# Block ends of a graph attention: the residual comes through an adding transfer instead of a VectorE pass

## The chip, the cores and the metric

The kernel runs on one core of a Trainium2 chip. The metric is device time in microseconds (us) of one execution. Before the change three runs took 1257.01, 1259.73 and 1262.62 us, with a median of 1259.73. One execution was also recorded by the hardware profiler, with the start and end of every instruction and DMA packet.

The engines are named as in the profile: PE is TensorE (matmuls), PEld its weight loads, DVE is VectorE, ACT is ScalarE, POOL is GpSimd and SP is SyncE, which here only issues transfers. Each engine works through its own queue in order.

## The reference

One layer has two parts. The first is a graph attention over N = 4096 nodes with 4 heads of 64 columns, the second a mixture of 8 experts with the best two for each node.

```python
h = einsum('nd,hdk->hnk', x, W)                      # x is layer-normed first
e = leaky_relu(s_row[:, :, None] + s_col[:, None, :], 0.2)
e = where(adj[None] > 0, e, -9e15)
out = einsum('hij,hjk->hik', softmax(e), h)          # then heads side by side: N x 256
residual = x @ Wr + br
y = elu(out) + residual
y = gamma * (y - mean(y)) / sqrt(var(y) + 1e-5) + beta
x = x + y                                            # then layer norm, top-2 gate, experts, x + sum
```

The change concerns the line `y = elu(out) + residual` and the row totals that the following layer norm needs. The exponential linear unit is written as max(y, 0) + exp(-relu(-y)) - 1; the -1 is already in the stored residual.

## The kernel before, in words

The rows of the attention are worked in four blocks a = 0 to 3 of 1024 rows, each in two halves of 512. Within a block a loop over j = 0 to 31 runs over 128 neighbours at a time. In each step VectorE makes four weight tiles `w` of 128x1024 (L1689, one per head, 10 buffers), ScalarE makes the mask (L1606) from an adjacency tile loaded by SP, and TensorE adds up 16 products for the rows (`acc`, L1198) and 8 for the softmax denominators (`den`, L1207), each recorded as two matmuls, so 48 records a step.

When a block's sums are complete, `finish_blocks` (L1393) ends it: divide by the denominators, the unit, the residual, two layer norms, storing the rows, choosing experts, and writing the rows into lists per expert in HBM (L1385, 16 scatters on POOL). It is a generator: each `next(pending)` (L1739) runs it up to the next `yield`, once for each step j of the following block. So the end of blocks 0, 1 and 2 lies spread over the loops a = 1, 2 and 3. The last block is ended by another function in the expert stage, which the change leaves alone. With the 26 yields of a block end (29 for the first block), of which one is taken at the block's boundary, the last piece with the scatters is traced at step 25 (28).

A scheduler orders each engine's queue ahead of time, by a cost model, from the order of tracing as priority and from readiness. TensorE's attention and block-end work is tied to the order of tracing by `queue` (L529) through `order_of` (L543); the other engines' work may be moved.

Tiles come from pools with a fixed number of buffers: `loaded` (L239) has two, `large` (L233) three. In a block end `rb` (the residual rows, loaded on SP by L1417) and later `xf` (x plus beta, L1439 to L1441) take turns in `loaded`; `y` of both halves and the scratch `m` are the three of `large`. There are adding transfers in the kernel already: L1441 adds x from HBM to a copy of beta, and L1450 adds `xf` to `y` within SBUF.

In loop a = 3 three more things matter. At step 3 `plan_early` (L1744) puts many small VectorE instructions beside the end of block 2. The expert stage starts behind the loop, with the first tile's rows already loaded at step 3. Its next rows, `early` (L571, from `load_full`, L1997), are loaded by SP once the lists are written, and transposed on TensorE (L607) before the products of the stage's first job (L1907) go on. `fetch` (L1777) loads each job's bias (L1792) and weights (L600, L1799) on the same SP queue.

Of the kernel before, what the change touches and what calls it, by code (L numbers as in the profile page):

```python
# [13 lines left out]
AF = mybir.ActivationFunctionType  # L14
OP = mybir.AluOpType
# [29 lines left out]
def gat_then_moe(  # L45
# [19 lines left out]
    nc = tc.nc  # L65
# [8 lines left out]
    HB = 2  # L74
# [34 lines left out]
    residual = nc.dram_tensor("residual", [N, D], F32, kind="Internal").ap()  # L109
# [39 lines left out]
    def rows_of(mat, b):  # L149
        return mat[ts(b, B), :].rearrange("(t p) d -> p t d", p=P)  # L150
# [50 lines left out]
    def sums_of(name, n=TB):  # L201
        return small.tile([P, n], F32, tag=name, name=name)

    def squares(square, src, off, junk):

        for t in range(TB):
            nc.scalar.activation(  # L207
                junk[:, t, :], src[:, t, :], AF.Square, bias=off[:, t : t + 1],
                accum_out=square[:, t : t + 1],
            )  # L210

    def means(total):

        off = sums_of("off", HB * TB)
        nc.vector.tensor_scalar(off, total, -1.0 / D, None, op0=OP.mult)  # L215
        return off


    def forward(apart, stack):
# [13 lines left out]
        def large(name):  # L233
            return home[0].tile([P, TB, D], F32, tag="large", name=name, bufs=3)
# [4 lines left out]
        def loaded(name):  # L239
            return fin.tile([P, TB, D], F32, tag="loaded", name=name, bufs=2)  # L240
# [4 lines left out]
        def bank(shape, name):  # L245
            return ps.tile(shape, F32, tag="bank", name=name, bufs=3)
# [296 lines left out]
        def order_of(ins):  # L543

            if ordered[0] or strict[0]:
                queue(ins)
            return ins.ins
# [67 lines left out]
        with ExitStack() as layer:  # L615
# [620 lines left out]
            def shares_of(pd):  # L1236

                z = small.tile([P, TB, H, HB], F32, tag="z", name="z")
                for h in range(0, H, 2):
                    nc.vector.reciprocal(z[:, :, h : h + 2], pd[:, :, PLACE[h] : PLACE[h] + 2, :HB])  # L1240
                return z
# [151 lines left out]
            def finish_blocks(a):  # L1393

                u = fin.tile([P, HB, H // 2, B], F32, tag="u", name="u", bufs=1)
                ud = fin.tile([P, B], F32, tag="ud", name="ud", bufs=1)

                nc.scalar.activation(ud, den, AF.Identity, bias=tiny)
                for i in reversed(range(H // 2)):
                    for half in range(HB):  # L1400
                        nc.scalar.activation(  # L1401
                            u[:, half, i], acc[half][i], AF.Identity, bias=hbar[:, i : i + 1]
                        )
                yield
                pd = bank([P, TB, H, Q], "pd")
                for t in range(TB):
                    order_of(nc.tensor.transpose(
                        pd[:, t].rearrange("p h q -> p (h q)"), ud[:, ts(t, P)], ident
                    ))
                z = shares_of(pd)  # L1410
                xe = rows_listed()
                n = HB * TB
                halves = [(half, slice(half * TB, (half + 1) * TB)) for half in range(HB)]
                rbs, ys, xbs = [], [], []
                for half, here in halves:
                    rbs.append(loaded("rb"))
                    nc.sync.dma_start(rbs[-1], rows_of(residual, a * HB + half))  # L1417
                for half, here in halves:
                    ys.append(large("y"))
                    results_of(ys[half], u[:, half], z[:, :, :, half])  # L1420
                    yield
                m = large("m")
                total = sums_of("total", n)
                for half, here in halves:
                    y = ys[half]
                    nc.scalar.activation(m, y, AF.Relu, scale=-1.0)
                    nc.scalar.activation(m, m, AF.Exp, scale=-1.0)
                    nc.vector.scalar_tensor_tensor(y, y, 0.0, m, op0=OP.max, op1=OP.add)
                    for t in range(TB):
                        nc.vector.scalar_tensor_tensor(  # L1430
                            y[:, t, :], y[:, t, :], 0.0, rbs[half][:, t, :], op0=OP.add, op1=OP.add,
                            accum_out=total[:, half * TB + t : half * TB + t + 1],
                        )
                    yield
                off = means(total)
                square = sums_of("square", n)
                for half, here in halves:
                    squares(square[:, here], ys[half], off[:, here], m)
                    xbs.append(loaded("xf"))  # L1439
                    nc.scalar.copy(xbs[half], bet.unsqueeze(1).to_broadcast([P, TB, D]))  # L1440
                    nc.gpsimd.dma_start(xbs[half], rows_of(x, a * HB + half), accum_op=OP.add)  # L1441
                    yield
                r = rstd_of(square, n, 1.0 / D)
                nc.vector.tensor_tensor(off, off, r, OP.mult)
                yield
                for half, here in halves:
                    y = ys[half]
                    normal(y, y, off[:, here], r[:, here])
                    nc.vector.tensor_tensor(y, y, gam.unsqueeze(1).to_broadcast([P, TB, D]), OP.mult)
                    nc.gpsimd.dma_start(y, xbs[half], accum_op=OP.add)  # L1450
                    yield
                yield
                total = sums_of("total", n)
                for half, here in halves:
                    for t in range(TB):
                        nc.scalar.activation(
                            m[:, t, :], ys[half][:, t, :], AF.Identity,
                            accum_out=total[:, half * TB + t : half * TB + t + 1],
                        )
                    nc.gpsimd.dma_start(rows_of(out, a * HB + half), ys[half])  # L1460
                    yield
                off = means(total)
                square = sums_of("square", n)
                for half, here in halves:
                    squares(square[:, here], ys[half], off[:, here], m)
                    yield
                r = rstd_of(square, n, 1.0 / D)
                nc.vector.tensor_tensor(off, off, r, OP.mult)
                yield
                for half, here in halves:  # L1470
                    normal(xe[:, here, :D], ys[half], off[:, here], r[:, here])
                    yield
                yield from route_rows(a * HB, xe)

            def rows_listed():
                return fin.tile([P, HB * TB, RW], F32, tag="xe", name="xe", bufs=1)

            def normal(into, src, off, r):

                for t in range(TB):  # L1480
                    nc.scalar.activation(
                        into[:, t, :], src[:, t, :], AF.Identity,
                        bias=off[:, t : t + 1], scale=r[:, t : t + 1],
                    )

            def results_of(y, u, z):

                pts = [bank([P, 2, HK], "ptr") for t in range(0, TB, 2)]
                for t in range(TB):
                    for i in range(H // 2):  # L1490
                        order_of(nc.tensor.transpose(  # L1491
                            pts[t // 2][:, t % 2, ts(i, P)], u[:, i, ts(t, P)], ident
                        ))
                for t in range(TB):
                    for h in range(H):
                        nc.scalar.activation(
                            y[:, t, ts(h, K)], pts[t // 2][:, t % 2, ts(h, K)], AF.Copy,
                            scale=z[:, t, h : h + 1],
                        )
# [110 lines left out]
            if not apart:  # L1610

                with tc.tile_pool(name="gen", bufs=2) as work:
# [12 lines left out]
                    for b in range(NB):  # L1625
# [4 lines left out]
                        for j in range(NT):  # L1630
# [6 lines left out]
                            for h in range(H):  # L1637
                                nc.vector.scalar_tensor_tensor(
                                    top[:, h, :], off, eb[:, j, h : h + 1], top[:, h, :],
                                    op0=OP.add, op1=OP.max,  # L1640
# [5 lines left out]
                            mx, mx, SLOPE, mx, op0=OP.mult, op1=OP.max  # L1646
                        )
                        for j in range(NT):
# [7 lines left out]
                            for h in range(H):  # L1656
                                nc.vector.tensor_scalar(
                                    w[:, h, :], rows[:, h, :], eb[:, j, h : h + 1], None,
                                    op0=OP.add,
                                )  # L1660
                            nc.vector.scalar_tensor_tensor(
                                w, w, SLOPE, w, op0=OP.mult, op1=OP.max
# [7 lines left out]
                        if b % HB == HB - 1 and b + 1 < NB:  # L1670
                            for _ in finish_blocks(b // HB):
                                pass
# [437 lines left out]
```

## Time and profile before

| what | value |
|---|---|
| profiled execution, whole time | 1258.36 us |
| its span, first to last instruction | 1256.7 us |
| median of three runs | 1259.73 us |
| TensorE busy | 1239.8 us (99%) |
| VectorE busy | 845.1 us (67%) |
| ScalarE busy | 448.2 us (36%) |
| GpSimd busy | 241.3 us (19%) |
| w tiles of VectorE, L1689 | 496 of 1.275 us |
| mean HBM traffic | 148 GB/s |

The attention loops a = 1, 2 and 3 run from about 250 to 777 us in the profile, the expert stage from 777 to the end. In a row of the profile, "x6: 1214/1222/1224" gives the count and the least, median and greatest duration in ns. Some rows name what ended an engine's idle time before an instruction. A window row gives the length of a stretch and then each engine's busy time in it with its count of instructions, the granted TensorE clock, the busy share of the DMA engines and GB/s. The chain of waits is the list of pieces that ended last, followed back from the last instruction: start, length, what. A busy TensorE row can include waiting within overlapping matmuls, so busy time alone doesn't tell the rate.

### The profile page before, as it was taken

The page shows a single profiled execution, that of the slowest core. Times are in us where ns is not written, and L with a number is a line of the kernel's source. Part 1 is how long each engine was busy: PE and PEld are TensorE (multiplying, and loading weights), DVE is VectorE, ACT ScalarE, POOL GpSimd, SP SyncE. Part 2 cuts the span into 40 slices and gives each one's busy share as a digit, 9 for nine tenths or more (in the row PEclk, how much of TensorE's full clock was granted, in tenths as well). Part 3 has the DMA queues.
Part 4 walks back from the last instruction along what each step waited for, and adds up shares of the span by engine and source line. Part 5 has one row for each costly group of instructions (what it writes and reads, how often), then busy time and mean ns, then how long its engine had stood idle before and what let it go on. Part 6 is the DMA issues. An engine that isn't in the chain of part 4 may idle for free.

```text
span 1256.7 us, 22720 instructions
## 1 busy us (share of the span) xinstructions
PE 1239.8 (99%) x8872; PEld 647.8 (52%) x8872; DVE 845.1 (67%) x1566; ACT 448.2 (36%) x918; POOL 241.3 (19%) x217
## 2 busy tenths in 40 slices
PE   9999999999999999999999999999999999999997
PEld 5444444332232332332325334888888876666686
DVE  7998887879999989999999996845111211111120
ACT  4332322265522375322655232533332332222322
POOL 4000000001002601006110024135222212122222
PEclk9999999999999999999999999999999999999999
DMA  6333533436533646335375423868898897455662
GB/s 215 118 119 110 167 111 102 157 113 139 181 110 107 224 116 201 107 98 157 112 171 191 122 84 103 269 181 230 218 234 213 215 229 144 106 139 106 138 161 36
DMA packets 155541, 190.23 MB, mean 151 GB/s; under 512 B 72312, under 2 KB 125680, under 8 KB 155040
## 3 DMA queue, kind: packets, MB, share of 16 engines
q1 hardware_dynamic: 133392, 145.39, 39.8%
q0 software_dynamic: 20544, 36.74, 13.2%
q10 hardware_dynamic: 1488, 6.55, 1.4%
q8 instruction: 71, 1.16, 0.4%
q14 instruction: 46, 0.38, 0.1%
HBM read 155.77 MB, written 29.74 MB: 148 GB/s over the span
## 4 chain that ended last, share of the span: by engine, by line
PE 93%; DVE 3%; issue 1%; ACT 1%; DMA 1%; another core or an unknown queue 0%; POOLq 0%; SPq 0%; DVEq 0%; ACTq 0%
PE acc L1198 33%; PE po L1907 18%; PE ph L1873 17%; PE den L1207 17%; PE pr L1053 2%; DVE w L1689 2%; PE ph L1101 2%; PE ptx L1253 0%; DMA early<-lists 0%; PE acc L894 0%; PE pt L780 0%; PE ptr L1491 0%; PE po L1946 0%; PE pl L1264 0%; PE po L875 0%
## 5 line engine op out<-in xcount | busy, mean ns | idle before, releaser
L1198 PE MATMUL acc<-w,ha 128*32 128x512 f32 x4096 | 669.9, 593 | 1.3 <-ACT u L1401 0.9
L1689 DVE SCALAR_TENSOR_TENSOR w<-er,eb,am 128x1024 f32<-128x1024 f32 x496 | 606.1, 1275 | 31.1 <-PE den L1207 31.1
L1207 PE MATMUL den<-w,unit 128*2 128x512 f32 x2048 | 466.9, 592 | 0.1
L1198 PEld LDWEIGHTS acc<-w,ha 128*32 128x32 f32 x4096 | 184.5, 110 | 292.8 <-issue 253.9
L1606 ACT ACTIVATE am<-adj 128x1024 bf16<-128x1024 int32 x124 | 130.6, 1054 | 346.5 <-DVE w L1689 211.7
L1873 PE MATMUL ph<-xT,w 128*128 128x256 f32 (+5 forms) x864 | 231.4, 425 | 2.9 <-ACT hT L1877 2.6
L1907 PE MATMUL po<-w,hT 128*128 128x256 f32 (+1 forms) x1040 | 230.2, 380 | 0.0
L1877 ACT ACTIVATE hT<-ph,bias 128x256 f32<-128x256 f32 (+5 forms) x216 | 111.1, 517 | 292.8 <-issue 185.7
L1907 PEld LDWEIGHTS po<-w,hT 128*128 128x128 f32 (+1 forms) x1040 | 196.2, 189 | 31.5 <-issue 3.1
L1873 PEld LDWEIGHTS ph<-xT,w 128*128 128x128 f32 x864 | 163.8, 191 | 63.4 <-issue 38.7
L1920 DVE SCALAR_TENSOR_TENSOR o<-po,share,b2s 128x256 f32<-128x256 f32 (+2 forms) x66 | 31.5, 479 | 230.1 <-PE po L1907 186.4
L1207 PEld LDWEIGHTS den<-w,unit 128*2 128x2 f32 x2048 | 93.5, 85 | 148.2 <-issue 139.8
L1932 POOL DMA_INDIRECT out<-o,ids x66 | 102.3, 1550 | 325.0 <-DMA out<-o,ids 151.0
L1385 POOL DMA_INDIRECT lists<-xe,at x64 | 89.0, 1391 | 268.0 <-issue 184.8
L1857 DVE STREAM_TRANSPOSE xT<-xr 128x512 f32<-128x512 f32 (+5 forms) x21 | 17.9, 851 | 57.1 <-PE ph L1873 31.2
L1053 PE MATMUL pr<-wr,xT 128*128 128x256 f32 x128 | 30.4, 381 | 0.2 <-ACT er L1147 0.2
L1895 ACT ACTIVATE b2s<-b2b,share 128x256 f32<-128x256 f32 x68 | 30.0, 498 | 0.0
L1121 POOL DMA_DIRECT2D residual<-rb x6 | 4.7, 784 | 121.2 <-DVE rb L1068 121.2
L1441 POOL DMA_DIRECT2D xf<-in_x x6 | 8.1, 1351 | 102.2 <-ACT xf L1440 102.2
L1053 PEld LDWEIGHTS pr<-wr,xT 128*128 128x128 f32 x128 | 24.1, 190 | 5.4 <-issue 0.9
L1101 PE MATMUL ph<-wall,xT 128*128 128x264 f32 x96 | 24.6, 399 | 0.0
L207 ACT ACTIVATE m<-y,off 128x256 f32<-128x256 f32 x48 | 23.7, 495 | 1.1 <-DVE off L215 0.6
(394 smaller groups left out, 617.9 us busy)
## 6 DMA issues: line engine op xcount, KB each, us to landing
adj<-in_adj SPq DMA_DIRECT2D x126, 512.0 KB
w<-in_L_ffn_W SPq DMA_DIRECT2D x54, 1024.0 KB
er<-parts ACTq DMA_DIRECT2D x3, 2048.0 KB
lists<-zeros POOLq DMA_DIRECT2D x8, 520.0 KB
residual<-rb POOLq DMA_DIRECT2D x8, 512.0 KB
rb<-residual SPq DMA_DIRECT2D x8, 512.0 KB
out<-y POOLq DMA_DIRECT2D x8, 512.0 KB
xb<-in_x SPq DMA_DIRECT2D x7, 512.0 KB
```

The costliest lines, as they stand in the source:

```text
L1053: order_of(nc.tensor.matmul(pr[:, k, :], turned[b][:, c, ts(t0 + k, P)], wr[:, c, :], start=(c == 0), stop=(c == DC - 1),))
L1101: order_of(nc.tensor.matmul(phs[t - t0], xT[:, c, ts(t, P)], wall[:, c, :], start=(c == 0), stop=(c == DC - 1),))
L1198: queue(nc.tensor.matmul(acc[half][h // 2][here : here + Q, :], ha[:, j, h * K + g * Q : h * K + (g + 1) * Q], w[half][h], start=(j == 0), ...
L1207: queue(nc.tensor.matmul(den[here : here + HB, :], unit[:, j, h, 1 - half : 1 - half + HB], w[half][h], start=(j == 0 and half == 0), stop ...
L1385: ins = nc.gpsimd.indirect_dma_start(lists, bass.IndirectOffsetOnAxis(ap=at[:, k, t : t + 1], axis=0), xe[:, t, :], None,).ins
L1606: nc.scalar.activation(am, at, AF.Relu, scale=2.0)
L1689: marks["w"] = nc.vector.scalar_tensor_tensor(wh[:, these], er[:, these, h], eb[:, j, h : h + 1], mask[:, these], op0=OP.max, op1=OP.min,).ins
L1873: order_of(nc.tensor.matmul(ph, job["w1"][:, c, ts(f, P)], xT[:, c, :], start=(c == 0), stop=(c == DC - 1),))
L1877: job["gelu"] = nc.scalar.activation(hT[:, f, :], ph, AF.Gelu, bias=job["bias"][:, f : f + 1]).ins
L1907: order_of(nc.tensor.matmul(po[:size], hT[:, f, k * CH : k * CH + size], w2[:, f, :], start=(f == 0), stop=(f == FC - 1),))
L1920: given_out.append(nc.vector.scalar_tensor_tensor(o[:size], po[:size], share[:size, k : k + 1], b2s[k][:size], op0=OP.mult, op1=OP.add,).ins)
L1932: added.append(add().ins)
```

## The change

Each half's exponential is made in a tile of its own from `loaded`, and a DMA issued on GpSimd adds the residual rows from HBM to it. Then four row passes of VectorE compute max(y, 0) plus that tile and take the row totals in the same instruction. The SP loads of `rb` and the VectorE pass over the whole half that put the unit together are gone. The making of the exponentials and the row passes are now two loops with a yield in each turn, where before they were one: two yields more per block end. `m`, still the scratch of the later square sums, is taken after them.

```diff
-                rbs, ys, xbs = [], [], []
-                for half, here in halves:
-                    rbs.append(loaded("rb"))
-                    nc.sync.dma_start(rbs[-1], rows_of(residual, a * HB + half))
+                ms, ys, xbs = [], [], []
                 for half, here in halves:
                     ys.append(large("y"))
                     results_of(ys[half], u[:, half], z[:, :, :, half])
                     yield
-                m = large("m")
                 total = sums_of("total", n)
                 for half, here in halves:
+                    ms.append(loaded("m"))
+                    nc.scalar.activation(ms[half], ys[half], AF.Relu, scale=-1.0)
+                    nc.scalar.activation(ms[half], ms[half], AF.Exp, scale=-1.0)
+                    nc.gpsimd.dma_start(
+                        ms[half], rows_of(residual, a * HB + half), accum_op=OP.add
+                    )
+                    yield
+                for half, here in halves:
                     y = ys[half]
-                    nc.scalar.activation(m, y, AF.Relu, scale=-1.0)
-                    nc.scalar.activation(m, m, AF.Exp, scale=-1.0)
-                    nc.vector.scalar_tensor_tensor(y, y, 0.0, m, op0=OP.max, op1=OP.add)
                     for t in range(TB):
                         nc.vector.scalar_tensor_tensor(
-                            y[:, t, :], y[:, t, :], 0.0, rbs[half][:, t, :], op0=OP.add, op1=OP.add,
+                            y[:, t, :], y[:, t, :], 0.0, ms[half][:, t, :], op0=OP.max, op1=OP.add,
                             accum_out=total[:, half * TB + t : half * TB + t + 1],
                         )
                     yield
+                m = large("m")
                 off = means(total)
                 square = sums_of("square", n)
```

## The prediction

> **What bounds the kernel now.** I read the page first, then the windows, the chain, the waits around a block end, and the rows of the lines that the diff touches. The page puts TensorE far ahead:
>
> ```profile
> PE 1239.8 (99%) x8872; PEld 647.8 (52%) x8872; DVE 845.1 (67%) x1566; ACT 448.2 (36%) x918; POOL 241.3 (19%) x217
> ...
> L1689 DVE SCALAR_TENSOR_TENSOR w<-er,eb,am 128x1024 f32<-128x1024 f32 x496 | 606.1, 1275 | 31.1 <-PE den L1207 31.1
> ```
>
> TensorE is without a record for 1256.7 - 1239.8 = 16.9 us in all. VectorE's long group waits 31.1 us, all of it for TensorE. But busy matmul records can hide slow stretches, so I took the start times of the matmul records of L1198 and L1207 from TensorE's timeline and counted them off in 48s, one step j of the attention each. An undisturbed step takes 5.15 us. With matmuls of a block end inside it takes 5.6 to 6.7, and in a=1 and a=2 no other step from j=2 on is over 5.17. Only a=3 differs: step 5 (from 631.4) takes 5.57, step 9 (from 652.4) 5.89, step 10 5.30: 0.42 + 0.74 + 0.15 = 1.31 us over 5.15. There VectorE also has the early plan. The chain of waits shows the same place:
>
> ```profile
> 592.75 1.72 PE acc L1198 x16
> 609.65 1.85 PE acc L1198 x16
> 630.95 8.36 DVE w L1689 x7
> 639.40 2.60 DVE w L1689 x3
> 648.14 2.39 DVE w L1689 x2
> 701.25 1.85 PE acc L1198 x16
> ...
> 772.07 1.72 PE acc L1198 x16
> 779.18 5.86 DMA early<-lists
> 787.25 6.91 PE po L1907 x32
> ```
>
> So VectorE carries the chain once, from 613 to 655, and at 779 a load of listed rows does. In windows of 10 us from 240 to 780 TensorE lacks 0.92 us at 250 (ScalarE's copies) and this:
>
> ```profile
> 640.00:650.00 10.00, 10.00 (x100) 2.96 (x96) 10.00 (x14) 4.78 (x8) 0.00 (x0) 1.00 0.43 129
> 650.00:660.00 10.00, 9.59 (x88) 2.97 (x84) 10.00 (x10) 5.67 (x15) 2.50 (x3) 1.00 0.70 145
> ```
>
> The third and fourth columns are span and TensorE, then weight loads, VectorE. How close VectorE is: from the end of each w to the first matmul that reads it, the smallest distance in a step stays above 1.31 us in a=1 and 1.11 in a=2 (both at step 10), and falls to 0.05 in a=3.
>
> **What the Trainium skill says.** "Trainium Kernel Development and Optimization", Best Practices: matmul busy share is no measure of the distance to the limit; hence the step spacing above, which showed 0.9 us of stretching that the busy time hides. "DMA: Bandwidth & Descriptors", SWDGE vs HWDGE vs iDMA: accumulating in a DMA needs GpSimd's software path; the trace agrees, both kinds of adding transfer here (L1441, L1450) are issued on POOL. The same page, Anatomy of one DMA, fits 2.0 us plus bytes at 436 GB/s, so an estimate of 3.2 us for 512 KB; the trace says longer: from issue to last landing L1441 took 5.8 to 7.2 us. I use 6.2, that of the first in a=3. "GPSIMD Engine Reference", Specifications: GpSimd shares its SBUF interfaces with VectorE instructions that have two SBUF inputs. The trace agrees: a scatter of L1385 takes up to 2.09 us beside VectorE's w, and 0.96 to 1.00 after 846, when no w runs.
>
> **Part by part.** Per half of a block end:
>
> ```profile
> L1428 DVE SCALAR_TENSOR_TENSOR y<-y,m x6: 1214/1222/1224, 277.5 to 626.6; 128x1024 f32<-128x1024 f32 x6
> ...
> L1430 DVE SCALAR_TENSOR_TENSOR y<-y,rb x24: 410/417/422, 279.8 to 628.9; 128x256 f32<-128x256 f32 x24
> L1430 DVE DVE_READ_ACCUMULATOR y<-y,rb x24: 74/80/84, 280.2 to 629.3; 128x1 f32 x24
> ```
>
> *Removed*: the pass of L1428, 6 x 1.222 = 7.3 us of VectorE, 2.44 per block end. The four row passes keep shape, operand count and row sums; max in place of add, so 0.417 + 0.080 us as now. In a=1 and a=2 TensorE is the cover and nothing is gained. In a=3 2.44 exceeds the 1.31 us of stretching: gain at most 1.31, or 1.7 if the 0.41 us by which step 17 exceeds its like in a=1 (6.70 against 6.29) goes too.
>
> *Removed*: six loads of 512 KB on SyncE (0.38 us issue each). *Added*: six adding transfers of 512 KB on POOL, at L1441's 1.35 us issue. Same bytes from HBM. ScalarE keeps its two passes (1.11 + 1.06); the second half's no longer waits for L1428 (0.3 us, once). POOL waits for the exponential with the transfer, and nothing is queued behind: before L1441 it idles 26.1 us in a=3. Block 0's scatters end at 431.9, inside a=2, and some 442 after the shift below, before that loop's first exponential is ready at 450.5.
>
> *Added wait*: VectorE's row passes wait for the transfer, with the w of the next steps queued behind them and TensorE behind those. In a=3 the first exponential ends at 622.2, so the sum lands near 622.3 + 6.2 = 628.5. The pass is traced two steps later, but VectorE runs ahead: by 622.5 it has done the w of step 4. If the scheduler puts the pass right there, VectorE stands 6.0 us; if it allows for the landing, 0. At 6.0 the loss is 6.0 - 2.44 = 3.6 in a=3, 3.6 - 1.31 = 2.3 in a=1 and 3.6 - 1.11 = 2.5 in a=2: 8.3 us. The lower end is the gain of 1.7. I take 2 us of standing: L1428, traced at step 2, was itself put where its inputs were ready, behind the w of step 4. Then a=1 and a=2 lose nothing and a=3 keeps 1.31 + 2 - 2.44 = 0.87 of stretching: gain 0.4. If the scheduler allows for the landing the gain is 1.3; I book 0.9, the middle.
>
> *Moved*: two more yields, so all behind the sums comes two steps later, 2 x 5.15 = 10.3 us: adds, stores, route transposes (TensorE's order is fixed by trace order here), ranks and the 16 list scatters. A block end takes 28 of 32 steps then, 31 for a=0, so it fits. SyncE's two xf loads, issued as buffers come free (657.5, 662), move too, past adjacency loads that ScalarE does not wait for now. What is late next is the scatter of a=3 before the expert stage:
>
> ```profile
> 770.20 0.97 POOL L1385 DMA_INDIRECT lists<-xe,at  x1 [0.30 <-issue]
> 777.34 0.97 POOL L493 MEMSET zeros<- 128x1040 f32 x1 [6.17 <-PE den L1207]
> ```
> ```profile
> 778.01 0.39 SPq L1799 DMA_DIRECT2D w<-in_L_ffn_W  x1
> 779.18 0.38 SPq L571 DMA_DIRECT2D early<-lists  x1
> ```
>
> Its last packet lands at 772.8, and SyncE passes waits on all eight counters of GpSimd's DMAs at 778.9: 6.1 us of slack. The first scatter, at 745.5, moves to 745.5 + 10.3 - 0.9 = 754.9. Up to VectorE's last w (767.6 - 0.9) the pitch stays that of now, 12 in 20.6 us, so seven go; nine follow at 1.27 us as after 846, and the last, issued near 777.1, lands 2.6 us later as now, at 779.7, against SyncE at 778.0: 1.7 us late. The load itself landed at 785.0 because 1 MB of weights (778.0) was ahead of it until 784.3; it still has that cover. TensorE took it up 0.44 us late now, at 786.1. I book +0.3; without the weights ahead it would be 1.7.
>
> Sum: -0.9 + 0.3 = -0.6 us. The profiled execution took 1258.36 (span 1256.7 and 1.7 around it), so 1257.8; it lay 1.4 below the median of the three runs, 1259.73. On that median: **1259.1 us**.
>
> **Rivals.** (1) *The transfer is the new wait.* It takes the place of L1428 on VectorE, 2 to 8.3 us as worked out, about 1264 at 4 us net. For it: the slack of 0.05 to 1.3 us. Against: ten microseconds of trace distance. (2) *Slower, by the order on SyncE.* If the scheduler believes the scatter later than SyncE's turn, it lets the bias and both weight loads of job 1 go ahead of the first early load. Those landed up to 793.9, so early rows come 793.9 - 785.0 = 8.9 us later, and TensorE, whose transposes of these rows are in line ahead of L1907, stands for it: 1259.73 - 0.9 + 8.9 = 1267.7. It decides as soon as the scatter is modelled past about 779; the shift leaves 1.7 us on the wrong side by my count, but the order stored now is trace order. (3) *Faster by over 0.5%.* VectorE's freed time would have to return 6.3 us of TensorE; waits for VectorE sum to 1.7, and the rest of the 16.9 us lies in the opening and the expert stage, which have no L1428. At 7 us: 1252.7. (4) *The change doesn't do what it says*: the row passes get slower and eat the 2.44; time as now, 1259.7.
>
> **Numbers.** Likeliest (small gain, all hidden, with rival 4): 0.68, own range 1256.5 to 1261.5. Transfer wait: 0.14, nearly all within 0.5%. SyncE order: 0.12, mostly above. Faster: 0.06. A difference of 0.5% (6.3 us) is about what a measurement of this kernel tells from none; the three runs spread 5.6. So faster 0.06, same 0.82, slower 0.12. The range takes the likeliest, most of rival 1 and the runs' spread: 1254.5 to 1266.
>
> **What would show it.** L1428 gone; 24 row passes near 0.42 us; six adding transfers from the residual landing in 6 to 7 us; steps of 5.15 us at 631 and 652; the last scatter 4 to 10 us later; the first early load still straight behind the first weights and landing by 786. VectorE idle for a DMA ahead of the row passes would speak for rival 1, weights ahead of early rows for rival 2. I am wrong if the attention's steps with no transposes change by more than 0.1 us each, since then TensorE was not the limit.

## The result, and the profile after

The changed kernel takes 1279.45 us in the median of six runs (1274.14 to 1284.25), the kernel before on the same chip 1258.37 (1255.72 to 1262.62). The ratio is 1.017 with a 95% interval of 1.0148 to 1.0192: slower by about 21 us, where 1259.1 and no change were predicted. The profiled execution took 1284.25 us with a span of 1282.5, so it is the slowest of the six; its span is 25.8 us longer than that of before.

The page of the changed kernel answers the lines shown of before. The third line is the share of each engine in the chain that ended last.

```profile
PE 1252.0 (98%) x8872; PEld 661.7 (52%) x8872; DVE 839.4 (65%) x1560; ACT 447.3 (35%) x918; POOL 243.5 (19%) x223
...
PE 60%; issue 17%; DVE 12%; DMA 4%; ACT 4%; POOL 2%; another core or an unknown queue 1%; POOLq 0%; SPq 0%; ACTq 0%; DVEq 0%
...
L1198 PE MATMUL acc<-w,ha 128*32 128x512 f32 x4096 | 675.5, 594 | 8.8 <-DVE w L1691 6.9
L1691 DVE SCALAR_TENSOR_TENSOR w<-er,eb,am 128x1024 f32<-128x1024 f32 x496 | 605.0, 1275 | 24.9 <-PE den L1207 24.5
```

In the chain TensorE had 93% and VectorE 3% before; now VectorE, DMA and "issue", time in which an engine waits for nothing that the profile shows, hold a third of it. VectorE is busy 5.7 us less (839.4 against 845.1), and yet TensorE now waits 6.9 us for its `w` tiles in the group of L1198 alone. Busy time of TensorE rose by 12 us for the same 8872 matmuls: it again includes waiting.

The row passes have become L1431. Their row names what VectorE sat idle for. Before, VectorE's waits list only one for an instruction of a block end, 0.2 us of L1428 for ScalarE:

```profile
L1431 DVE SCALAR_TENSOR_TENSOR y<-y,m x24: 415/418/426, 281.8 to 650.1; 128x256 f32<-128x256 f32 x24
L1431 DVE DVE_READ_ACCUMULATOR y<-y,m x24: 78/82/86, 282.1 to 650.4; 128x1 f32 x24
...
  DMA m<-residual: 18.7, 3
```

The passes are as long as before (0.418 and 0.082 us), but VectorE stands (is idle for the transfer) 18.7 us in three places, once per block end. VectorE's timeline in a=1 shows the first (the bracket gives the idle time before the instruction and its cause):

```profile
269.79 4.87 DVE L1691 SCALAR_TENSOR_TENSOR w<-er,eb,am 128x1024 f32<-128x1024 f32 x4 [1.68 <-PE den L1207]
274.58 0.22 DVE L262 COPY bT<-pb 128x64 f32<-128x64 f32 x1
281.80 0.42 DVE L1431 SCALAR_TENSOR_TENSOR y<-y,m 128x256 f32<-128x256 f32 x1 [7.00 <-DMA m<-residual]
```

The `w` of the next steps are queued behind this pass. The chain of waits, taken between 270 and 290 us, holds the transfer itself, and again in a=3, where `w` of VectorE carries the chain for long after it:

```profile
272.86 8.83 DMA m<-residual
...
281.76 5.86 issue
...
287.63 6.61 DMA xf<-in_x
...
629.79 8.12 DMA m<-residual
...
652.81 2.48 DVE w L1691 x2
...
656.47 3.91 DVE w L1691 x4
...
661.26 3.67 DVE w L1691 x3
```

In the windows shown of before TensorE had 10.00 and 9.59 us of 10; now, with the loop a=3 starting 13.4 us later, it has less, and it lacks time again from 670 to 680 (9.12):

```profile
640.00:650.00 10.00, 9.52 (x92) 3.23 (x88) 10.00 (x39) 2.92 (x3) 1.28 (x1) 1.00 0.73 136
650.00:660.00 10.00, 9.11 (x84) 2.47 (x80) 10.00 (x13) 5.86 (x18) 1.28 (x1) 1.00 0.86 224
```

The smallest distance in a step from the end of a `w` to the first matmul that reads it, VectorE's lead from here on, tells the same: at step 4 of a=1 it was 7.52 us, and is 0.99 now; at steps 10 to 15 it is 0.05, so TensorE waits for VectorE there.

The table puts the span between landmarks of TensorE: the start of a=1, the start of the last attention step (a=3, j=31), the first matmul of the expert stage, and the 401st. Last column: the rest. (The recorded expectations count the last step to its own last matmul instead: 4.7 us before and 8.4 after the change, where the table has 5.26 and 8.89.)

| us | to a=1 | a=1 to last step | last step | expert stage, first 400 matmuls | rest |
|---|---|---|---|---|---|
| before | 256.19 | 515.69 | 5.26 | 77.33 | 402.23 |
| changed | +1.26 | +15.35 | +3.63 | -0.07 | +5.63 |
| changed, executed again | -0.43 | +14.98 | 0.00 | +3.47 | -4.47 |

The second line of the changed kernel is the run after_again, told below. The 1.26 us ahead of a=1, where nothing was changed, come with a granted clock of 0.50 for 3.4 us from 8.2 on. What comes back in both is 15 us in the attention and 3.5 us where the attention ends. The rest of the expert stage differs by 10 us between two executions with nothing changed, so it is not counted as an effect of the change (the last section shows where the 10 us lie); the same column goes from -4.5 to +5.6 over all runs below with this data.

### The profile page after: what moved, and what is told of

Same layout as the page of the kernel before. It is cut to its first block, busy times and chain, and to the rows that moved or that the text cites. A ratio compares the mean times of both kernels' runs of the same rounds, so it can differ in the third digit from the quotient of the medians.

```text
span 1282.5 us, 22725 instructions
## 1 busy us (share of the span) xinstructions
PE 1252.0 (98%) x8872; PEld 661.7 (52%) x8872; DVE 839.4 (65%) x1560; ACT 447.3 (35%) x918; POOL 243.5 (19%) x223
## 4 chain that ended last, share of the span: by engine, by line
PE 60%; issue 17%; DVE 12%; DMA 4%; ACT 4%; POOL 2%; another core or an unknown queue 1%; POOLq 0%; SPq 0%; ACTq 0%; DVEq 0%
PE ph L1875 17%; PE po L1909 16%; PE acc L1198 14%; DVE w L1691 10%; PE den L1207 7%; DMA y<-xf 2%; POOL lists L1385 2%; DMA m<-residual 2%; PE pr L1053 1%; PE ph L1101 1%; ACT m L207 1%; ACT am L1608 1%; DMA xf<-in_x 1%; ACT y L1498 1%
## 5 line engine op out<-in xcount | busy, mean ns | idle before, releaser
L1198 PE MATMUL acc<-w,ha 128*32 128x512 f32 x4096 | 675.5, 594 | 8.8 <-DVE w L1691 6.9
L1207 PE MATMUL den<-w,unit 128*2 128x512 f32 x2048 | 474.1, 592 | 1.8 <-issue 1.1
L1198 PEld LDWEIGHTS acc<-w,ha 128*32 128x32 f32 x4096 | 187.5, 110 | 304.5 <-issue 233.2
L1385 POOL DMA_INDIRECT lists<-xe,at x64 | 83.1, 1298 | 281.1 <-issue 101.8
L1101 PEld LDWEIGHTS ph<-wall,xT 128*128 128x128 f32 x96 | 17.2, 189 | 12.6 <-issue 10.2
```

The costliest lines, as they stand in the source:

```text
L1101: order_of(nc.tensor.matmul(phs[t - t0], xT[:, c, ts(t, P)], wall[:, c, :], start=(c == 0), stop=(c == DC - 1),))
L1198: queue(nc.tensor.matmul(acc[half][h // 2][here : here + Q, :], ha[:, j, h * K + g * Q : h * K + (g + 1) * Q], w[half][h], start=(j == 0), ...
L1207: queue(nc.tensor.matmul(den[here : here + HB, :], unit[:, j, h, 1 - half : 1 - half + HB], w[half][h], start=(j == 0 and half == 0), stop ...
L1385: ins = nc.gpsimd.indirect_dma_start(lists, bass.IndirectOffsetOnAxis(ap=at[:, k, t : t + 1], axis=0), xe[:, t, :], None,).ins
```

## Experiments

Theory A: the row passes stand in VectorE's order ahead of the landing of the transfer, VectorE stands, and its lead is gone for the rest of the block end. Theory B: the two yields more, which move everything behind them by two steps, cost the time.

**Row passes behind the newest w.** In the changed kernel; `issue_after` puts the row passes behind the newest `w` in VectorE's order.

```diff
+                    with tc.issue_after(marks["w"]) if apart else nullcontext():
                         for t in range(TB):
                             nc.vector.scalar_tensor_tensor(
```

> The changed kernel with one edit: the four row passes of each half are tied behind the newest w tile on VectorE, so that those of half 0 stand two w (2.4 us) later in VectorE's order than in the changed kernel. Theory A (VectorE stands for the adding transfer because its row passes are ordered ahead of the landing, and this standing stalls TensorE through the rest of the block end): the standing falls from 7.0, 6.3 and 5.4 us to about 4.6, 3.9 and 3.0, and the three attention loops lose about half of the 15.4 us that the changed kernel lost there: 1264 to 1273 us, between before and changed. Theory B (the two further yields, which move everything behind them two steps later, cost the time): the standing falls, but the time stays that of the changed kernel, 1276 to 1283.

1270.89 us against 1259.41 of before, ratio 1.010 (1.0064 to 1.0136). VectorE's waits in a=1 of this kernel (total, times, longest):

```profile
DVE w L1692 <- PE den L1207: 6.4, 3, 3.2
DVE y L1432 <- DMA m<-residual: 2.9, 1, 2.9
DVE off L215 <- ACT m L1459: 2.5, 1, 2.5
DVE v L155 <- ACT m L207: 0.9, 1, 0.9
```

The standing is 2.9, 2.5 and 1.8 us, 7.1 in all in place of 18.7, and the stretch from a=1 to the last step loses 6.99 us in place of 15.35. The standing fell by more than two `w`: between the copy ahead of it and these `w` VectorE waited 1.5 us for TensorE in any case. Half of the loss goes with the standing, as theory A says, but the other half is not lost where VectorE stands: in a=1 and a=2 it begins at step 12, beside the wait for ScalarE's row totals (L1459 here, 2.5 and 2.9 us), and a=3, which has the standing and not that wait, loses nothing. That wait returns below. The last step keeps its 3.66.

**The same, one yield later.** A bare `yield` ahead of the loop of row passes is added to the kernel above.

> As the run with the row passes tied behind w, with one more yield ahead of the row-pass loop: the row passes of half 0 stand about 7 us later than in the changed kernel, and the rest of the block end three steps later than before instead of two. Theory A: the standing is 0 to 1 us per block end, the attention loops are back at their time before (within 2 us), and what may stay is what happens at the end of the last loop and in the expert stage (0 to 6 us): 1257 to 1266. Theory B: a third step of shift makes it worse than the changed kernel, 1280 to 1290.

1271.45 us, ratio 1.0093 (1.0057 to 1.013), above the 1257 to 1266 expected. VectorE stands nowhere for the transfer, and the stretch from a=1 to the last step is 516.96 us, 1.27 over before. So the standing was the cause there. But the end got worse: the last step takes 9.72 us more than before (up to 1.7 of it by a granted clock of 0.50 for 3.4 us from 782.0 on). The time that the first gave back was lost by the second, which is the part of theory B that holds.

**The yields alone.** In the kernel before:

```diff
+                yield
+                yield
                 m = large("m")
```

> The kernel before with two bare yields ahead of its scratch tile m, and nothing else: the shift of the changed kernel without its transfer. Theory A: the attention loops a=1 to a=3 keep their time (within 2 us); the scatters of the last loop run to its end, which may cost 0 to 5 us in the last attention step and in the expert stage: 1257 to 1265. Theory B: most of the loss is here: 1270 to 1280.

1264.78 us, ratio 1.0043 (1.0027 to 1.006). From a=1 to the last step +0.33 us, the last step +3.64. The yields hardly change the loops and cost about 4 us at the end. In a=3 they alone bring the stretched steps 5, 9 and 10 back to 5.15 us, at 0.59 us more in steps 11 and 12: those 1.31 us needed no VectorE work taken away.

**The pass taken out alone.** In the kernel before; the exponential is left out of the sum.

```diff
-                    nc.vector.scalar_tensor_tensor(y, y, 0.0, m, op0=OP.max, op1=OP.add)
...
-                            y[:, t, :], y[:, t, :], 0.0, rbs[half][:, t, :], op0=OP.add, op1=OP.add,
+                            y[:, t, :], y[:, t, :], 0.0, rbs[half][:, t, :], op0=OP.max, op1=OP.add,
```

> The kernel before with the VectorE pass of L1428 taken out and the row passes computing max(y, 0) plus the loaded residual: the exponential is still made on ScalarE but is left out of the sum, so the output lacks it. Loads on SyncE, yields and order stay. It measures what the removal of 2.44 us of VectorE per block end is worth without the transfer: by both theories 0.5 to 1.7 us less than before, all of it in a=3 around steps 5 to 10, so 1256 to 1259, not to be told from before. If it were 4 us or more faster, VectorE would be more of a limit than the slack of before says.

1303.39 us, ratio 1.035 (1.0312 to 1.0388), a miss of the expectation that has nothing to do with VectorE: other values choose other experts, and the stage then loads 56 weight tiles instead of 54 and takes 46.7 us longer behind its 400th matmul. Up to the expert stage the run can be read: a=1 and a=2 take exactly what they took (174.95 and 171.72 us), a=3 1.71 us less, the stretched steps 5, 9 and 10 are at 5.15, and step 17 is as in a=1. So 1.7 us is all that the removal is worth up to there.

**Late row passes without a shift.** In the kernel with the extra yield, three yields are taken out further on:

```diff
                 nc.vector.tensor_tensor(off, off, r, OP.mult)
-                yield
...
                     squares(square[:, here], ys[half], off[:, here], m)
-                    yield
+                yield
...
                 nc.vector.tensor_tensor(off, off, r, OP.mult)
-                yield
```

> The kernel with late row passes (tied behind w, one more yield ahead of them), with three yields taken out further on (behind each of the two products of off and r, and between the halves of the second square sums), so that the scatters are traced at the same step as in the kernel before. Theory A: no standing for the transfer, attention loops from the start of a=1 to the last step within 2 us of the 515.7 before; the last step and the expert stage as before, since the scatters are over in time: 1257 to 1261 in all. If the last step is long again (over 6 us against 4.7) although the scatters end before it, the late scatters are not its cause. Theory B (the transfer itself costs, wherever the row passes stand): 1265 or more.

1257.0 us against 1256.64 of before, ratio 1.0002 (0.999 to 1.0015). All parts of the change are in this kernel. From a=1 to the last step it takes 514.72 us, 0.97 less than before, the last step 5.26 as before. Its page and the windows:

```profile
PE 91%; DVE 4%; ACT 1%; DMA 1%; issue 1%; POOLq 0%; SPq 0%; DVEq 0%; ACTq 0%
```
```profile
640.00:650.00 10.00, 10.00 (x100) 2.93 (x96) 10.00 (x11) 5.94 (x18) 0.00 (x0) 1.00 0.67 165
650.00:660.00 10.00, 10.00 (x96) 2.90 (x92) 9.96 (x15) 4.88 (x7) 0.00 (x0) 1.00 0.37 116
```

TensorE has both windows whole. The smallest lead of a=1 rose from 1.31 us (step 10) to 2.55 (step 15). The first halves' transfers still land only 8.2 to 8.8 us after issue. So the transfer costs nothing where its users stand late enough, and the freed VectorE time is lead that TensorE has little use for.

**The yields in the first two block ends only.** The kernel before, with `if a + 2 < NR:` ahead of the two bare yields.

> The kernel before with the two bare yields in the ends of blocks 0 and 1 only; the end of block 2, in the last attention loop, keeps its place. If it is the scatters of block 2, running beside the last attention step, that cost 3.6 us there, the last step takes 4.7 us again, and the time is that before: 1258 to 1261. If the last step still takes 8 us, it is something else that the yields move.

1257.48 us, ratio 1.0014 (1.0002 to 1.0025); the last step is 5.26 us again. What the yields cost is tied to the end of block 2, whose scatters are the last ahead of the expert stage.

**More w behind the last step.** The kernel with two bare yields; `weigh` is called twice more behind the last step of a=3, eight tiles that nobody reads.

> The kernel with two bare yields, and behind the last attention step eight more w tiles on VectorE that nobody reads (extra work, no change of the output). Where VectorE makes w, scatters follow each other at up to 2.39 us, without it at 1.27. If it is the dense row of scatters beside an idle VectorE that starves TensorE in the last step, the step falls from 8.4 us to near 4.7 to 6, while the scatters end some 4 us later and the first rows of the expert stage with them: 1258 to 1266. If the density does not matter, the last step stays at 8 us or more, and the time at 1264 to 1270.

1261.83 us, ratio 1.0034 (1.0022 to 1.0046). The last step fell to 5.26 us, but the first 400 matmuls of the expert stage took 6.42 more: TensorE stood 3.6 us for rows of the lists, since SyncE had waited 3.6 us for scatters. TensorE takes up these rows at 790.4, in a stretch with a granted clock of 0.50 from 789.0 to 795.8, and half of the 5.4 us left of that makes 2.7 us more. By the expectation the short last step speaks for the dense row of scatters as its cause; the second execution of the changed kernel, below, takes that reading away, since there the last step is short with nothing filled in.

**Transfers in four pieces.** In the changed kernel:

```diff
-                    nc.gpsimd.dma_start(
-                        ms[half], rows_of(residual, a * HB + half), accum_op=OP.add
-                    )
+                    for t in range(TB):
+                        nc.gpsimd.dma_start(
+                            ms[half][:, t], rows_of(residual, a * HB + half)[:, t],
+                            accum_op=OP.add,
+                        )
```

> The changed kernel with each adding transfer of 512 KB made as four of 128 KB, one for each row pass, at the same places. If the landing time goes with the bytes of one transfer, the first row pass stands 3 to 4 us instead of 7.0 and the others follow as their pieces land, so the standing falls by 1 to 3 us per block end: 1268 to 1277. If it goes with the descriptors or with what else is in the queues, the last piece lands as late as before or later: 1277 to 1290.

1287.84 us, ratio 1.0249 (1.0232 to 1.0266). In a=1 the first half stands 4.0 and then 1.1 us in place of 7.0: the pieces do land earlier, 5.85 to 6.81 us after issue. But GpSimd's order changed with it:

```profile
271.46 3.63 POOL L1425 DMA_DIRECT2D m<-residual  x4 [34.38 <-PE pb L261]
281.82 1.30 POOL L1445 DMA_DIRECT2D xf<-in_x  x1 [6.74 <-ACT xf L1444]
282.77 3.91 POOL L1425 DMA_DIRECT2D m<-residual  x4
```

The second half's pieces now stand behind the `xf` transfer of the first half, which waits for the first half's row passes. So the second half makes VectorE stand too, 5.5 us in a=1, and the attention loses 24.8 us, up to 1.7 of it because the granted clock was 0.5 for 3.4 us from 296.7 on. What splitting alone is worth stays open.

**The changed kernel without the shift.** Two yields are taken out of it, behind each `off, off, r` product; the row passes stay where they are.

> The changed kernel with two yields taken out further on (behind each of the two products of off and r), so that its scatters are traced at the same step as before, while the row passes stay where VectorE stands for the transfer. Theory A, in parts: the standing stays at about 18.7 us in all and the attention from the start of a=1 to the last step at 530 to 532 us (before 515.7, changed 531.0); the last step falls from 8.4 to 4.7 us. Together 15 to 16 us over before, give or take the 5 us by which the expert stage varies: 1269 to 1277. If the last step stays long, the shift is not its cause; if the attention loops lose less than 12 us, the yields had a part in that loss.

1264.74 us against 1254.09, ratio 1.0082 (1.0065 to 1.0099): 10.7 us over before, where 15 to 16 were expected. The last step is 5.26 us again. The standing is the same (18.6 us), but from a=1 to the last step it loses 11.05 us and not 15.35, 1.70 of it in step 0 of a=1, where the block end has not reached the transfer and the granted clock is 0.50 for 3.4 us from 258.7 on. VectorE's waits in a=2, first of the changed kernel, then of this one:

```profile
DVE y L1431 <- DMA m<-residual: 6.3, 1, 6.3
DVE off L215 <- ACT m L1458: 2.9, 1, 2.9
DVE w L1691 <- PE den L1207: 1.7, 1, 1.7
DVE v L155 <- ACT m L207: 0.9, 1, 0.9
```
```profile
DVE y L1431 <- DMA m<-residual: 6.3, 1, 6.3
DVE w L1689 <- PE den L1207: 3.0, 6, 1.7
DVE r L159 <- ACT s L157: 0.7, 1, 0.7
```

So by my expectation theory A was not the whole of the attention's loss. In the changed kernel VectorE also stands 2.9 us for ScalarE's row totals (L1458). In its order in a=1 and a=2 the two passes with gamma (L1451) have four `w` between them; the second half's adding transfer, and the totals behind it, start that much later. In this kernel, in that before, and in that with the two yields alone, there is one `w` between them, and the wait is missing; so it is missing in a=3 of the changed kernel. Only runs with both the transfer and the shift have it. In the kernel with late row passes and the shift the same wait shows. In a=1 (2.5 us) that loop loses only 0.14 us: without the standing the lead covers it. In a=2 it is longer (4.0 us), and that loop loses 1.77.

**The changed kernel again.** Nothing is edited.

> The changed kernel once more, with nothing edited, to see which parts of its loss come back in a second execution. Theory A: the standing (7.0, 6.3, 5.4 us) and the lengths of the attention steps agree within 0.3 us, the last step is near 8.4 us again. If the 5 us in the expert stage between 77 and 104 us after its first matmul are a matter of the single execution, they are different here (0 to 9 us); if they belong to the kernel, 5 to 6 us again.

1271.92 us in one run. The standing is 7.0, 6.3 and 5.3 us and the attention steps agree within 0.12 us, but for 0.47 us in step 31 of a=2 and for the last one. The last step takes 5.26 us this time, not the 8.9 of the first execution, and the 3.5 us are lost behind it. The 5.6 us that the first execution lost further on in the expert stage did not come back. The chain of waits there, and SyncE's and GpSimd's timelines:

```profile
792.39 7.79 DMA lists<-xe,at
...
800.39 2.69 DMA early<-lists
...
804.11 0.70 DVE y L1544
...
804.85 0.44 PE pt L607 x2
```
```profile
792.02 0.34 SPq L1794 DMA_DIRECT2D b2b<-in_L_ffn_b  x1
792.57 0.39 SPq L1801 DMA_DIRECT2D w<-in_L_ffn_W  x1
800.39 0.38 SPq L571 DMA_DIRECT2D early<-lists  x1
```
```profile
791.12 0.97 POOL L1385 DMA_INDIRECT lists<-xe,at  x1 [0.30 <-issue]
792.39 0.97 POOL L1385 DMA_INDIRECT lists<-xe,at  x1 [0.30 <-issue]
```

The last scatter is issued at 792.39, beside the 1 MB of weights at 792.57, and lands after 7.79 us, where that of the kernel before took 2.59 with nothing beside it. SyncE holds the load of the early rows until then, and TensorE stands 3.2 us for them. In the first execution TensorE was slow in its last step instead, until 797.4; the weights were issued 3.75 us behind the last scatter (798.20 and 794.45), and the load was in time:

```profile
794.45 0.97 POOL L1385 DMA_INDIRECT lists<-xe,at  x1 [0.30 <-issue]
797.52 0.97 POOL L493 MEMSET zeros<- 128x1040 f32 x1 [2.10 <-PE den L1207]
```
```profile
798.20 0.39 SPq L1801 DMA_DIRECT2D w<-in_L_ffn_W  x1
799.36 0.38 SPq L571 DMA_DIRECT2D early<-lists  x1
```

In both executions 3.5 us are gone. Over all runs the place is the same: in the five other kernels whose scatters reach into the last step, that step and the 400 matmuls behind it together take 3.6 to 9.6 us more. In the five whose scatters are all issued before it starts, that before among them, the step takes 5.26 us.

## Why the prediction was wrong

- **What bounds the kernel.** Right. TensorE sets the pace, and taking the pass out gives 1.71 us in a=3 and nothing in a=1 and a=2; I had bounded it by 1.31, and by 1.7 with step 17. In the placing that costs nothing 0.97 us of it came back.
- **Row passes, transfers, POOL.** Right. 0.418 and 0.082 us a pass, six transfers at 1.29 to 1.39 us of issue, and nothing queued behind them was late.
- **Added wait: the step that failed.** I named the queue behind the waiting pass and priced standing from 0 to 6.0 us, 8.3 in sum, but took 2 us. It was 7.0, 6.3 and 5.4. Two terms were wrong. The landing: 8.83, 7.98 and 8.12 us for the first halves, not the 6.2 of another transfer, with an adjacency load ahead of it in the DMA engines; that put even my upper end of 6.0 too low for a=1 and a=2. And the placing: I set "ten microseconds of trace distance" against the wait, but trace distance did not delay the passes. They stood ahead of step 4's last two `w`, behind its first two, as L1428 had stood behind the `w` of step 4 for inputs that were in fact ready.
- **The sum made of it.** Sound with the right size: standing less 2.44 less the slack gives 7.0 - 2.44 - 1.31 = 3.25, 6.3 - 2.44 - 1.11 = 2.75 and 5.4 - 2.44 = 2.96 us, 9.0 in all. Without the shift the loops lost 9.35 us beside step 0 of a=1: 2.92, 2.72 and 3.71. So a=3 lost 0.75 more than this sum gives.
- **A term that was left out.** The two yields and the transfer together: another order in the same block end, with a later wait of VectorE for ScalarE (2.6 and 2.9 us in a=1 and a=2), which meets a lead that the standing has used up. It takes the attention's loss from 9.35 to 15.35 us. Why the scheduler chose that order stays open. I asked what is late next only at the scatters, not in the rest of the same block end.
- **Moved.** The count was right: with the yields alone the first scatter went to 755.77 and the last to 777.69, and I had written 754.9 and 777.1. The price was wrong: +0.3, as "it still has that cover", against 3.5 to 4 us. I took the weights as cover for the early load. In the second execution of the changed kernel, and in the run with more `w`, the last scatters landed late beside that 1 MB, and the load waited for them. In the first execution, and with the yields alone, the load was in time and TensorE was slow in the last step, for a reason that stays open.
- **Rivals.** Rival 1 was what happened, at more than its price (9.35 us against at most 8.3); its sign, VectorE idle for a DMA ahead of the row passes, is in the row of L1431. Rival 2 did not: the early load still stands right behind the first weights. The loss at the end lies where it pointed, but not by its mechanism.

Sum: 15 us in the attention and 3.5 at its end make 18.5 of the 21 us between the medians; the interval of the ratio goes down to 1.0148, or 18.6 us. What lies above is within what the expert stage varies by. The attention's part is shown by runs that take the standing and the shift away, one at a time and both; of the end, only the place is shown, and in one of two executions the wait.

## What to carry to other kernels

Before an engine is made to wait for a DMA, find where its waiting instruction stands in the stored order and count what is queued behind it: an engine with 7 us of lead lost it to one wait of 7 us, and got it back at 0.37 us per undisturbed step (0.45, 0.81, 1.18 and 1.54 us at steps 16 to 19 of a=1), so the next small waits cost as well. Take the landing time from a transfer that has the same loads ahead of it, and when a step moves, ask whether its own transfers now meet a big one. Where the pass that is taken away was hidden, as here, even a placing that costs nothing gave no gain that could be measured (ratio 1.0002).

## What the runs showed of the hardware

- In the changed kernel a 512 KB adding transfer landed 8.0 to 8.8 us after issue in the first halves and 6.0 to 6.1 in the second ones. The packet records of a=1 show the difference: those of the first (issued at 272.86) run from about 277 to 281, right behind an adjacency load that occupies the engines from 274 to 278, although SyncE issued that load 0.67 us after it; those of the second start about 2 us earlier after their issue, with no load ahead. "DMA: Bandwidth & Descriptors" of the Trainium skill, under Anatomy of one DMA, gives an estimate of 3.2 us for these bytes; the runs show about twice that without a load ahead. That the adjacency load makes the difference was not tested by moving it alone, but other runs agree. In the three kernels with row passes behind `w`, the second halves, too, have such a load issued 0.7 to 1.0 us behind them, and land in 8.0 to 9.7 us; one first half there, which has its load issued 1.3 us ahead of it, lands in 6.79.
- TensorE can be slow with no wait for another engine in the records: in the last step of the changed kernel the matmuls have gaps of up to 1.08 us named "issue", with clock 1.00 granted there, while scatters follow at 1.27 us. In the second execution of the same kernel there are none, with scatters at the same distance. No transfer of instructions is recorded in that step. What it is stays open.
- The expert stage behind its 400th matmul took 407.86 and 397.75 us in two executions of the changed kernel. Nearly all of the difference arises within 25 us. In the first execution TensorE waits there 3.75 and 2.64 us for ScalarE, and the granted clock is 0.50 for 3.4 us from 885.4 and again from 902.5, while that of the second execution is 1.00. The waits and half of TensorE's time at the lower clock make some 9.5 of the 10.1 us; the second execution has neither, and the kernel before one wait of 2.5 us and one such stretch (from 880.5). What ScalarE waited for in turn is not named in the records. So a stage of a single execution is compared only with its clock and waits at hand.
